# Carrying the last Gram products of a fused attention kernel into the pass over v

## The chip, the cores and the metric

The kernel runs on one core of a Trainium2 chip. Its metric is the device time of one execution in microseconds (us); the time before is 2299.94 us, the median of three runs (2297.13 to 2300.26). The engines are named as the profile names them: PE is TensorE (matmuls, with PEld its weight loads), DVE is VectorE, ACT is ScalarE, POOL is GpSimd, and SP is SyncE, which here only issues transfers. "q" behind a name (SPq, ACTq) is the queue of that engine's sequencer. Each engine works through its own instructions in the order in which they were laid down.

## The reference, cut to what matters

One image `x` of 384 channels and 192 x 192 pixels goes through two residual layers. Only the first is touched by the change:

```python
qkv = einsum('bchw,oc->bohw', groupnorm(x), w_qkv) + b_qkv   # 384 -> 1152 channels
qkv = qkv.reshape(..., 96, 2, 96, 2).max(axis=(3, 5))        # 2x2 max pooling
qkv = depthwise_conv3x3(qkv) + b_dw
q, k, v = split(qkv, 3)                                      # 8 heads of 48 channels
attn = (q/|q|) @ (k/|k|).T * temperature                     # over channels: 48 x 48 per head
out  = sum_i topk_softmax(attn, k_i) @ v * a_i               # k_i = 24, 32, 36, 38
x    = x + w_proj @ upsample2x(gelu(out)) + b_proj
```

The attention is over channels, so q and k are needed only through the 48 x 48 products q k^T of each head (the Gram matrices) and through the norms of their rows. The second layer is a group norm, a sign, a shift by channel and a product with the signs of a weight matrix.

## The kernel before, in words

The image is cut into 24 units of 8 rows (`NU`, 1536 pixels each); a unit of x is a tile of 128 partitions x 3 channel groups x 1536 pixels (2304 KB), held in the pool `big` of 8 buffers. There are four stages.

1. **Statistics** (0 to 160 us): all units are read for the group norm; the last six read stay in SBUF (`kept`).
2. **The q,k pass** (160 to about 1345 us): for each unit u and each of six groups of 128 output channels (m = 0 to 5), `qkv_unit` makes three blocks of 128 x 512 on TensorE (L321; three matmuls a block, each of which shows as two records), VectorE pools each block out of PSUM into a padded tile (L328), ScalarE adds the bias (L335) and makes the first tap of the depthwise convolution (L342), and VectorE makes the other eight taps (L344). Then `transposed` (L381, L384) writes 32 x 32 transposes into the tile `blocks`, and `moved` sends these through 32 transfers on SyncE's queue (L394 for q, L399 for k, sixteen each) into the tile `room`, where they form whole transposed operands. `products(u)` (L410) multiplies them into three PSUM tiles `gram` that accumulate over all units. It is called one unit late, behind m = 2 of the unit after, so that the moves have a good part of a unit to land. Only the last unit has no unit after it: its products are called directly behind its moves, and then L438 copies the Gram tiles to SBUF (`gsb`).
3. **The v pass** (about 1337 to 1990 us): the same for the three groups of v, without transposes; the result goes to `chunk`. From unit 1 on, `softmaxes` (a generator that makes one step after each m) turns the Gram matrices into the attention matrix, and `attention` applies it once it is there. At the start of this stage `w_projG` and `weightT` are loaded into one buffer `wl` one after the other (L574, L580, on ScalarE's queue), VectorE reduces the first (L575), and ScalarE takes the sign of the second (L581).
4. **Projection and second layer** (1990 us to the end).

Pools set much of what may overlap. SBUF pools of the side "right" are a stack: what is opened later takes the memory of what was closed. `p2w` holds the six padded tiles of q and k and `blocks`; when it closes, `p4w` (v's padded tiles and `wl`) and `p3` (the softmax's scratch) take its place, and their first writers wait for the last user of the memory that they take. In PSUM the q,k pass has five buffers for products of x (`p2qkv`) and three for the Gram tiles (`p2g`); the v pass has three (`p4qkv`), four for `attention` (`p4o`) and one for small things (`p3ps`).

Outside the parts written under a manual schedule, a scheduler lays down the order of each engine's instructions from the program's order, its priorities and its own estimate of when an instruction could run; the order in the source is therefore not always the order on the engine.

Of the kernel before, what the change touches and what calls it, by code (L numbers as in the profile page):

```python
# [10 lines left out]
F32 = mybir.dt.float32  # L11
# [7 lines left out]
PSUM = bass.MemoryType.PSUM  # L19

P = 128
C = 384
CT = C // P
# [5 lines left out]
GRP = 12  # L29
NG = C // GRP  # L30
NM = 3 * C // P
UR = 8
NU = H // UR
# [28 lines left out]
KEEP = 6  # L62
# [15 lines left out]
NP = C // PAIR  # L78
# [69 lines left out]
def conv_preact_kernel(ctx: ExitStack, tc: tile.TileContext, a: dict, out: bass.AP):  # L148
    nc = tc.nc
# [27 lines left out]
    def unit(u, pool=big, parts=1):  # L177
        xt = pool.tile([P, CT, UPX], F32, name="xt", tag="big")
        n = CT // parts
        for t in range(0, CT, n):  # L180
            nc.sync.dma_start(xt[:, t : t + n], xv[u][:, t : t + n])
        return xt
# [12 lines left out]
    def group_sums(ps, s):  # L195

        for t in range(CT):
            nc.tensor.matmul(ps, ind[:, t, :], s[:, t], start=(t == 0), stop=(t == CT - 1))  # L198
# [8 lines left out]
    def right(name, bufs=1, stack=att):  # L207
        return stack.enter_context(tc.tile_pool(name=name, bufs=bufs, side="right"))
# [87 lines left out]
    def padded(pool, n):  # L296


        ts = []
        for m in range(n):  # L300
            t = pool.tile([P, PR + 3, WP + 2], F32, name=f"pooled{m}")
            nc.gpsimd.memset(t[:, 0:2, :], 0.0)  # L302
            nc.gpsimd.memset(t[:, 2 : PR + 2, 0:1], 0.0)
            nc.gpsimd.memset(t[:, 2 : PR + 2, WP + 1 :], 0.0)
            nc.gpsimd.memset(t[:, PR + 2 :, :], 0.0)
            ts.append(t)
        return ts
# [38 lines left out]
            nc.scalar.copy(pl[:, 0:2, :], pl[:, PR : PR + 2, :])  # L346


    with tc.tile_pool(name="p2w", bufs=1, side="right") as wp, tc.tile_pool(
        name="p2t", bufs=2, side="right"  # L350
    ) as tp, tc.tile_pool(name="p2qkv", bufs=5, space=PSUM) as pqkv, tc.tile_pool(
        name="p2g", bufs=1, space=PSUM
    ) as pg:
        pool = padded(wp, 2 * CT)
        gram = [pg.tile([P, 512], F32, name=f"gram{t}") for t in range(CT)]


        size = -(-(PR + 1) * WP // P) * C
        blocks = wp.tile([P, 2, size], F32, name="blocks")
        nc.gpsimd.memset(blocks, 0.0)  # L360
        room = big.tile([P, CT, UPX], F32, name="room", tag="big").rearrange("p t n -> p (t n)")
        qkT = room[:, : 2 * size].rearrange("p (s n) -> p s n", s=2)

        def of_unit(u):

            lo, hi = rows(u)
            n = hi - lo + 1
            nk = -(-n * WP // P)
            q, k = qkT[:, 0, : nk * C], qkT[:, 1, : nk * C]
            return (  # L370
                n,
                nk,
                q.rearrange("p (t k c) -> p t k c", t=CT, k=nk),
                k.rearrange("p (b k c) -> p b k c", k=nk, c=B),
            )

        def transposed(u, s, t, acc):
            n, nk, *_ = of_unit(u)
            to = blocks[:, s, : nk * C].rearrange("p (j t k c) -> p t k j c", j=NBP, t=CT, c=B)[:, t]
            full, more = divmod(n * WP // B, NBP)  # L380
            nc.vector.transpose(to[:, :full], acc[:, : full * P].rearrange("p (k j c) -> p k j c", j=NBP, c=B))  # L381
            if more:
                src = acc[:, full * P : n * WP].rearrange("p (j c) -> p j c", c=B)
                nc.vector.transpose(to[:, full, :more], src)  # L384

        def moved(u, s):

            n, nk, q, k = of_unit(u)
            for j in range(NBP):
                src = blocks[:, s, j * nk * CT * B : (j + 1) * nk * CT * B]  # L390
                for i in range(NBP):
                    at, to = slice(i * B, (i + 1) * B), slice(j * B, (j + 1) * B)
                    if s == 0:
                        nc.sync.dma_start(  # L394
                            q[to].rearrange("p t k (i c) -> p i (t k) c", i=NBP)[:, i],
                            src[at].rearrange("p (m c) -> p m c", c=B),
                        )
                    else:
                        nc.sync.dma_start(  # L399
                            k[to].rearrange("p (t i) k c -> p i t (k c)", i=NBP)[:, i],  # L400
                            src[at].rearrange("p (t m) -> p t m", t=CT),
                        )

        def products(u):

            n, nk, q, k = of_unit(u)
            for i in range(nk):
                L = min(P, n * WP - i * P)
                for t in range(CT):
                    nc.tensor.matmul(  # L410
                        gram[t][:, : BN[t] * B],
                        q[:L, t, i],
                        k[:L, B0[t] : B0[t] + BN[t], i],
                        start=u == 0 and i == 0,
                        stop=u == NU - 1 and i == nk - 1,
                    )

        for u in range(NU):
            for v in range(u, min(u + KEEP + 1, NU)):
                if v not in kept:  # L420
                    kept[v] = unit(v)
            xt = kept.pop(u)
            lo, hi = rows(u)
            n = hi - lo + 1
            for m in range(2 * CT):
                acc = tp.tile([P, (PR + 1) * WP], F32, name="dw")[:, : n * WP]
                qkv_unit(pqkv, xt, u, m, pool[m], [(acc, 0, n)])
                transposed(u, *divmod(m, CT), acc)
                sq = tp.tile([P, (PR + 1) * WP], BF16, name="sq", bufs=1)
                nc.scalar.activation(sq[:, : n * WP], acc, AF.Square, accum_out=ssq[:, m, u : u + 1])  # L430
                if u and m == CT - 1:
                    products(u - 1)
                if m % CT == CT - 1:
                    moved(u, m // CT)
        products(NU - 1)
        for t in range(CT):
            at = D0[t] - B0[t] * B
            nc.vector.tensor_copy(gsb[:, t, : DN[t]], gram[t][:, at : at + DN[t]])  # L438

    wpr = ctx.enter_context(tc.tile_pool(name="wpr", bufs=1)).tile([P, CT, C], F32, name="wpr")  # L440
    nc.scalar.dma_start(wpr, a["w_projT"].rearrange("(t p) o -> p t o", p=P))
# [120 lines left out]

    chunk = []
    with ExitStack() as vs:
        wp = right("p4w", stack=vs)
        scratch = vs.enter_context(ExitStack())
        p3 = right("p3", stack=scratch)
        pqkv = vs.enter_context(tc.tile_pool(name="p4qkv", bufs=3, space=PSUM))
        po = vs.enter_context(tc.tile_pool(name="p4o", bufs=NP, space=PSUM))
        psp = vs.enter_context(tc.tile_pool(name="p3ps", bufs=1, space=PSUM))  # L570
        pool = padded(wp, CT)

        wl = wp.tile([P, CT, C], F32, name="wl")
        nc.scalar.dma_start(wl, a["w_projG"].rearrange("(t p) o -> p t o", p=P))  # L574
        nc.vector.tensor_reduce(wg1, wl.rearrange("p t (g c) -> p t g c", c=GRP), AX.X, ALU.add)  # L575
        bg = psp.tile([P, P], F32, name="p3ps")[:NG, :1]
        group_sums(bg, bpr.unsqueeze(2))
        nc.vector.tensor_scalar_mul(bg1, bg, -1.0 / GRP)
        wl = wp.tile([P, CT, C], F32, name="wl")
        nc.scalar.dma_start(wl, a["weightT"].rearrange("(t p) o -> p t o", p=P))  # L580
        nc.scalar.activation(wb, wl, AF.Sign, saturate=False)  # L581
# [20 lines left out]
                    nc.scalar.activation(chunk[c][to, t, cols], ps[src], AF.Gelu, accum_out=osum[to, t, g : g + 1])  # L602

        for u in range(NU):
            xt = unit(u)
            if u == NU - 1:
                kept[u] = xt
                for i, f in enumerate(FIRST):
                    kept[f] = unit(f, big if i else early)
            if u % UC == 0:  # L610
                chunk.append(big.tile([P, CT, CPX], F32, name="chunk", tag="big"))
            lo, hi = rows(u)
            first = PR * u - 2 + lo
            last = first + hi - lo
            for m in range(CT):
                parts = []
                for c in range(first // CR, last // CR + 1):
                    r0, r1 = max(first, c * CR), min(last, c * CR + CR - 1)
                    parts.append(
                        (chunk[c][:, m, (r0 - c * CR) * WP : (r1 + 1 - c * CR) * WP], r0 - first, r1 + 1 - r0)  # L620
                    )
                qkv_unit(pqkv, xt, u, 2 * CT + m, pool[m], parts)
                if u >= TOPK and steps is None:
                    steps = softmaxes(p3, psp)
                if steps:
                    if next(steps, 1):
                        steps = ()
                        scratch.close()
                        early = opened("p5x0", 1)
                elif steps == () and done < NAB - HOLD and (done + 1) * ABLK <= first * WP:  # L630
                    attention(done)
                    done += 1
# [216 lines left out]
```

## Time and profile before

| what | value |
| --- | --- |
| time, median of 3 runs | 2299.94 us |
| span of the profiled execution | 2297.4 us |
| TensorE busy | 2104.5 us, 92% |
| VectorE busy | 1903.4 us, 83% |
| ScalarE busy | 819.2 us, 36% |
| GpSimd busy | 211.2 us, 9% |
| products of x (L321), 3888 records | 1682.8 us |
| depthwise taps (L344) of q, k and of v | 709.1 and 370.7 us |
| pooling (L328), 648 instructions | 443.0 us |
| block moves to `room` | 768 transfers, 2.0 us to landing |

The page's row of slices cuts the span into 40 parts of 57.4 us and gives the busy share of each in tenths. The groups give for each line and operation the busy time, the mean duration of one instruction in ns, and the idle time of the engine just before them with what ended most of it. A timeline lists instructions in order of time, with equal ones that follow each other merged; its bracket has the idle time before and the releaser.

### The profile page before, as it was taken

How to read it: one execution, taken by the hardware profiler on the slowest of the kernel's cores; microseconds unless marked ns; L12 is line 12 of the kernel's file. 1: busy time of each engine (PE TensorE's matmuls, PEld its weight loads, DVE VectorE, ACT ScalarE, POOL GpSimd, SP SyncE). 2: the span in 40 equal slices, each digit the busy share in tenths (PEclk: the TensorE clock that was granted, in tenths of full speed). 3: DMA queues.
4: the chain of work that ended last, by engine and by line, in shares of the span. 5: the costliest groups of instructions: out<-in, count | busy, mean ns of one | idle time of the engine just before them, and what ended most of it. 6: DMA issues, size and time to landing. Idle time of an engine off the chain costs nothing.

```text
span 2297.4 us, 19469 instructions
## 1 busy us (share of the span) xinstructions
PE 2104.5 (92%) x6135; PEld 995.6 (43%) x6135; DVE 1903.4 (83%) x3269; ACT 819.2 (36%) x1418; POOL 211.2 (9%) x338
## 2 busy tenths in 40 slices
PE   1029999999999999999999969999999999989998
PEld 0014444444444444444444434443444444455554
DVE  4658888888888888888888958986787887889998
ACT  5532222222222222222222212225333233487775
POOL 0000000000000000000000000000000000286674
PEclk7559999999999999999999989999999999999999
DMA  9962222222222322222111154104221212289996
GB/s 398 418 256 62 63 65 69 87 80 70 63 67 67 101 69 68 62 69 65 21 27 25 21 175 161 42 2 204 83 82 56 110 42 83 83 330 398 423 414 247
DMA packets 208727, 300.30 MB, mean 131 GB/s; under 512 B 162000, under 2 KB 164848, under 8 KB 208624
## 3 DMA queue, kind: packets, MB, share of 16 engines
q1 hardware_dynamic: 197936, 243.46, 30.4%
q10 hardware_dynamic: 10688, 55.61, 5.9%
q8 instruction: 48, 0.79, 0.1%
q14 instruction: 55, 0.45, 0.1%
HBM read 213.68 MB, written 56.62 MB: 118 GB/s over the span
## 4 chain that ended last, share of the span: by engine, by line
PE 75%; DVE 11%; DMA 9%; ACT 2%; issue 1%; SPq 1%; ACTq 0%; POOLq 0%; POOL 0%; DVEq 0%
PE qkv L321 63%; DMA xt<-in_x_dram 6%; PE l1ps L734 4%; DVE chunk L344 4%; PE yps L552 3%; PE gram L410 3%; DVE pooled L328 2%; PE ops L592 2%; DVE xt L561 2%; DVE dw L344 1%; DMA out_dram<-xt 1%; ACT signs L714 1%; DVE stats L248 1%; DMA wl<-in_weightT_dram 1%; DMA wl<-in_w_projG_dram 1%
## 5 line engine op out<-in xcount | busy, mean ns | idle before, releaser
L321 PE MATMUL qkv<-xt,wq 128*128 128x512 f32 x3888 | 1682.8, 594 | 1.9 <-DVE pooled L328 1.6
L321 PEld LDWEIGHTS qkv<-xt,wq 128*128 128x128 f32 x3888 | 736.4, 190 | 922.4 <-issue 824.5
L344 DVE SCALAR_TENSOR_TENSOR dw<-pooled,small,dw 128x384 f32<-128x384 f32 (+2 forms) x1152 | 709.1, 616 | 118.4 <-ACT dw L342 93.7
L328 DVE TENSOR_REDUCE pooled<-qkv 128x128 f32<-128x512 f32 x648 | 443.0, 685 | 83.2 <-PE qkv L321 71.1
L344 DVE SCALAR_TENSOR_TENSOR chunk<-pooled,small,chunk 128x384 f32<-128x384 f32 (+3 forms) x696 | 370.7, 547 | 77.9 <-ACT chunk L342 60.3
L346 ACT COPY pooled<-pooled 128x196 f32<-128x196 f32 x207 | 73.6, 356 | 773.6 <-DVE dw L344 542.9
L335 ACT ACTIVATE pooled<-pooled,small 128x384 f32<-128x384 f32 x216 | 133.0, 616 | 408.2 <-DVE pooled L328 408.1
L714 ACT ACTIVATE signs<-xt,nmean 64x1536 fp8e4<-64x1536 f32 x144 | 226.5, 1573 | 62.5 <-PE yps L552 51.3
L734 PE MATMUL l1ps<-signs,wb 128*128 128x384 fp8e4 x864 | 151.5, 330 | 6.5 <-POOL signs L706 4.6
L561 DVE SCALAR_TENSOR_TENSOR xt<-yps,small,xt 128x768 f32<-128x768 f32 x132 | 127.9, 1013 | 23.8 <-PE yps L552 20.1
L742 DVE SCALAR_TENSOR_TENSOR xt<-l1ps,small,xt 128x768 f32<-128x768 f32 x144 | 135.7, 1009 | 7.1 <-ACT signs L714 4.0
L552 PE MATMUL yps<-chunk,wpr 128*128 128x384 f32 x396 | 136.5, 490 | 5.3 <-DVE xt L561 5.3
L248 DVE BATCH_NORM_STATS2 stats<-xt 128x6 f32<-128x512 f32 x144 | 87.2, 677 | 60.4 <-DMA xt<-in_x_dram 60.4
L302 POOL MEMSET pooled<- 128x196 f32 x9 | 2.4, 264 | 1351.5 <-DMA room<-blocks 1192.0
L198 PE MATMUL gsps<-sums,small 128*32 128x2 f32 x6 | 0.5, 196 | 128.2 <-DVE sums L269 128.2
L430 ACT ACTIVATE sq<-dw 128x384 bf16<-128x384 f32 (+2 forms) x144 | 75.3, 523 | 116.9 <-DVE dw L344 116.9
L734 PEld LDWEIGHTS <-wb 128*128 128x128 fp8e4 x864 | 84.4, 98 | 74.8 <-issue 17.3
L342 ACT ACTIVATE dw<-pooled,small 128x384 f32<-128x384 f32 (+2 forms) x144 | 100.5, 698 | 2.3
L552 PEld LDWEIGHTS yps<-chunk,wpr 128*128 128x128 f32 x396 | 72.6, 190 | 60.8 <-PE yps L552 16.4
L239 ACT ACTIVATE junk<-xt 128x1536 bf16<-128x1536 f32 x48 | 71.1, 1482 | 52.0 <-DMA xt<-in_x_dram 50.8
L381 DVE STREAM_TRANSPOSE blocks<-dw 128x384 f32<-128x384 f32 (+1 forms) x144 | 82.0, 569 | 3.5
L410 PE MATMUL gram<-room 128*128 128x160 f32 (+3 forms) x438 | 69.9, 315 | 12.4 <-DMA room<-blocks 12.4
(117 smaller groups left out, 642.1 us busy)
## 6 DMA issues: line engine op xcount, KB each, us to landing
xt<-in_x_dram SPq DMA_DIRECT2D x83, 2304.0 KB, 14.9
out_dram<-xt ACTq DMA_DIRECT2D x19, 2304.0 KB, 14.5
room<-blocks SPq DMA_DIRECT2D x736, 36.0 KB, 2.0
xt<-in_x_dram SPq DMA_DIRECT2D x18, 768.0 KB, 8.3
out_dram<-xt ACTq DMA_DIRECT2D x9, 768.0 KB, 8.0
out_dram<-xt SPq DMA_DIRECT2D x6, 768.0 KB, 6.6
wq<-in_w_qkvT_dram ACTq DMA_DIRECT2D x1, 1728.0 KB, 14.9
room<-blocks SPq DMA_DIRECT2D x32, 48.0 KB, 2.0
```

The costliest lines, as they stand in the source:

```text
L248: nc.vector.bn_stats(stats[b][:, t, at : at + 6], xt[:, t, j * 512 : (j + 1) * 512])
L321: nc.tensor.matmul(ps, wq[:, t, m * P : (m + 1) * P], x4[:, t, r0 : r0 + nr, c0 : c0 + ncol], start=(t == 0), stop=(t == CT - 1),)
L328: nc.vector.tensor_reduce(pl[:, 2 + r0 // 2 : 2 + (r0 + nr) // 2, 1 + c0 // 2 : 1 + (c0 + ncol) // 2], ps.rearrange("p (i a j b) -> p i j ...
L335: nc.scalar.activation(new, new, AF.Identity, bias=bq[:, m : m + 1])
L342: nc.scalar.activation(acc2, src, AF.Identity, bias=bdw[:, m : m + 1], scale=wdw[:, m, 0:1])
L344: nc.vector.scalar_tensor_tensor(acc2, src, wdw[:, m, k : k + 1], acc2, ALU.mult, ALU.add)
L410: nc.tensor.matmul(gram[t][:, : BN[t] * B], q[:L, t, i], k[:L, B0[t] : B0[t] + BN[t], i], start=u == 0 and i == 0, stop=u == NU - 1 and i ...
L552: nc.tensor.matmul(ps, wpr[:, t, m * P : (m + 1) * P], o[:, t, :], start=(t == 0), stop=(t == CT - 1),)
L561: nc.vector.scalar_tensor_tensor(x5[:, m, r], yb, bpr[:, m : m + 1], x5[:, m, r], ALU.add, ALU.add)
L714: nc.scalar.activation(rows_of(sg, p, SAT[t] - HSHIFT[t][h]), xt[p, t, :].rearrange("p (r w) -> p r w", w=W), AF.Sign, bias=nmean1[p, t : ...
L734: nc.tensor.matmul(ps[:, j, : 2 * W], wb[:, t, m * P : (m + 1) * P], rows_of(sg, slice(0, P), SAT[t])[:, r0 + 2 * j : r0 + 2 * j + 2], sta ...
L742: nc.vector.scalar_tensor_tensor(blk, ps[:, :, : 2 * W], bl1[:, m : m + 1], blk, ALU.add, ALU.add)
```

## The change

The edit has three parts that belong together.

- **The last unit's products move.** `products(NU - 1)` and the copies of the Gram tiles leave the end of the q,k pass and become a function `gathered`, called in the v pass behind m = 1 of its first unit, so that there is work for TensorE while the last moves are under way. The buffers of the Gram tiles therefore stay open into the v pass, and the pools `p4o` and `p3ps`, with the three small bias sums (`group_sums`), open only behind `gathered`.
- **One PSUM pool for products of x.** A pool `qkv` of three buffers serves both passes in place of `p2qkv` (five) and `p4qkv` (three).
- **v's first tiles and units are freed of the moves.** In `p2w`, `blocks` is laid down ahead of the padded tiles, so that what `p4w` overlaps is padded tiles and not `blocks`; `p4w` gets `reuse_waits="tile"`, by which a new tile waits for the users of the tiles whose memory it takes, not for the whole pool. The loop over x units in the q,k pass reads ahead past its end: the v pass's units 0 to 5 are loaded by its last six rounds and kept under the keys 24 to 29.

```diff
-    with tc.tile_pool(name="p2w", bufs=1, side="right") as wp, tc.tile_pool(
-        name="p2t", bufs=2, side="right"
-    ) as tp, tc.tile_pool(name="p2qkv", bufs=5, space=PSUM) as pqkv, tc.tile_pool(
-        name="p2g", bufs=1, space=PSUM
-    ) as pg:
-        pool = padded(wp, 2 * CT)
+    products_of_x = ctx.enter_context(ExitStack())
+    pqkv = products_of_x.enter_context(tc.tile_pool(name="qkv", bufs=3, space=PSUM))
+    last_products = products_of_x.enter_context(ExitStack())
+    pg = last_products.enter_context(tc.tile_pool(name="p2g", bufs=1, space=PSUM))
...
         blocks = wp.tile([P, 2, size], F32, name="blocks")
         nc.gpsimd.memset(blocks, 0.0)
+        pool = padded(wp, 2 * CT)
...
-            for v in range(u, min(u + KEEP + 1, NU)):
+            for v in range(u, u + KEEP + 1):
                 if v not in kept:
-                    kept[v] = unit(v)
+                    kept[v] = unit(v % NU)
...
+    def gathered():
         products(NU - 1)
         for t in range(CT):
             at = D0[t] - B0[t] * B
             nc.vector.tensor_copy(gsb[:, t, : DN[t]], gram[t][:, at : at + DN[t]])
+        last_products.close()
...
-        wp = right("p4w", stack=vs)
+        wp = vs.enter_context(tc.tile_pool(name="p4w", bufs=1, side="right", reuse_waits="tile"))
...
-        pqkv = vs.enter_context(tc.tile_pool(name="p4qkv", bufs=3, space=PSUM))
-        po = vs.enter_context(tc.tile_pool(name="p4o", bufs=NP, space=PSUM))
-        psp = vs.enter_context(tc.tile_pool(name="p3ps", bufs=1, space=PSUM))
+        vs.enter_context(products_of_x)
...
         for u in range(NU):
-            xt = unit(u)
+            xt = kept.pop(NU + u) if NU + u in kept else unit(u)
...
                 qkv_unit(pqkv, xt, u, 2 * CT + m, pool[m], parts)
+                if u == 0 and m == 1:
+                    gathered()
+                    po = vs.enter_context(tc.tile_pool(name="p4o", bufs=NP, space=PSUM))
+                    psp = vs.enter_context(tc.tile_pool(name="p3ps", bufs=1, space=PSUM))
+                    bg = psp.tile([P, P], F32, name="p3ps")[:NG, :1]
+                    group_sums(bg, bpr.unsqueeze(2))
+                    nc.vector.tensor_scalar_mul(bg1, bg, -1.0 / GRP)
```

More of the change, by code (lines that the diff above doesn't have):

```diff
@@ L346, in qkv_unit @@
             nc.scalar.copy(pl[:, 0:2, :], pl[:, PR : PR + 2, :])
+    products_of_x = ctx.enter_context(ExitStack())
+    pqkv = products_of_x.enter_context(tc.tile_pool(name="qkv", bufs=3, space=PSUM))
+    last_products = products_of_x.enter_context(ExitStack())
+    pg = last_products.enter_context(tc.tile_pool(name="p2g", bufs=1, space=PSUM))
     with tc.tile_pool(name="p2w", bufs=1, side="right") as wp, tc.tile_pool(
         name="p2t", bufs=2, side="right"
-    ) as tp, tc.tile_pool(name="p2qkv", bufs=5, space=PSUM) as pqkv, tc.tile_pool(
-        name="p2g", bufs=1, space=PSUM
-    ) as pg:
-        pool = padded(wp, 2 * CT)
+    ) as tp:
         gram = [pg.tile([P, 512], F32, name=f"gram{t}") for t in range(CT)]
@@ L575, in conv_preact_kernel @@
         nc.vector.tensor_reduce(wg1, wl.rearrange("p t (g c) -> p t g c", c=GRP), AX.X, ALU.add)
-        bg = psp.tile([P, P], F32, name="p3ps")[:NG, :1]
-        group_sums(bg, bpr.unsqueeze(2))
-        nc.vector.tensor_scalar_mul(bg1, bg, -1.0 / GRP)
         wl = wp.tile([P, CT, C], F32, name="wl")
```

## The prediction

> **What bounds the kernel now.** I read the page first: the slices of the span, then the groups.
>
> ```profile
> PE   1029999999999999999999969999999999989998
> L321 PE MATMUL qkv<-xt,wq 128*128 128x512 f32 x3888 | 1682.8, 594 | 1.9 <-DVE pooled L328 1.6
> ```
>
> TensorE is at 9 tenths in nearly every slice from the fourth on; the products of x (L321) are most of it and hardly wait. One hole stands in mid-span, at the 24th slice (57.4 us each). Splitting the span around it gives this table (length, then busy time of TensorE, its weight loads, VectorE, ScalarE, GpSimd; clock, DMA share, GB/s):
>
> ```profile
> 200.00:1340.00 1140.00, 1138.40 (x2927) 537.08 (x2926) 994.47 (x1684) 301.52 (x694) 0.00 (x0) 1.00 0.23 62
> 1340.00:1403.00 63.00, 41.16 (x110) 21.05 (x109) 30.71 (x67) 7.95 (x15) 2.37 (x14) 0.84 0.67 256
> 1403.00:1990.00 587.00, 585.27 (x1683) 252.00 (x1683) 487.73 (x1002) 193.27 (x438) 3.67 (x5) 1.00 0.21 79
> ```
>
> In the q,k pass TensorE is idle 1.6 of 1140 us, in the v pass 1.7 of 587. So TensorE sets the pace of both, VectorE (87% and 83%) rides along, and the only time to win or lose between them is the 21.8 us of idleness from 1340 to 1403, plus whatever slow restarts cost. The timeline of TensorE in that stretch (start, length, instructions, idle time before and its releaser):
>
> ```profile
> 1314.69 20.76 PE L321 MATMUL qkv<-xt,wq 128*128 128x512 f32 x48
> 1337.05 7.99 PE L321 MATMUL qkv<-xt,wq 128*128 128x512 f32 x18 [1.60 <-DVE pooled L328]
> 1357.49 6.04 PE L410 MATMUL gram<-room 128*128 128x160 f32 x24 [12.45 <-DMA room<-blocks]
> 1363.36 1.02 PE L321 MATMUL qkv<-xt,wq 128*128 128x512 f32 x2
> 1371.80 0.48 PE L198 MATMUL p3ps<-small 128*32 128x1 f32 x6 [7.41 <-DVE gsb L438]
> 1372.20 24.39 PE L321 MATMUL qkv<-xt,wq 128*128 128x512 f32 x52
> ...
> 1396.43 0.38 PE L460 MATMUL p3ps<-dg,ones 128*128 128x128 f32 x2
> 1396.65 1.88 PE L321 MATMUL qkv<-xt,wq 128*128 128x512 f32 x4
> 1400.15 0.49 PE L460 MATMUL p3ps<-dg,ones 128*128 128x128 f32 x2 [1.61 <-DVE dg L458]
> ```
>
> Four waits: 1.60 for a PSUM buffer, 12.45 for the last unit's block moves, 7.41 behind the copies of the Gram tiles, and 1.61 (then 0.36 at 1402.72) for VectorE's diagonal tiles. After 1403.05, 226 records follow without a gap. VectorE and the SyncE queue say why the first two long ones last:
>
> ```profile
> 1345.66 10.25 SPq L399 DMA_DIRECT2D room<-blocks  x16
> 1357.66 1.89 DVE L328 TENSOR_REDUCE pooled<-qkv 128x128 f32<-128x512 f32 x3 [11.87 <-DMA room<-blocks]
> 1369.69 1.35 DVE L575 TENSOR_REDUCE wg<-wl 128x96 f32<-128x1152 f32 x1 [8.24 <-DMA wl<-in_w_projG_dram]
> ```
>
> Sixteen moves leave one per 0.64 us and each lands some 2 us later: 1345.66 + 10.25 + 1.4 = 1357.3. VectorE stands 11.87 us because v's pooled tiles reuse the memory of `blocks`, and 8.24 us at the reduction of w_projG, whose load took 12.1 us among six x loads. The Gram copies (L438) stand behind that reduction in VectorE's order, and TensorE's 7.41 us hangs on them.
>
> [...]after the 7.41 us gap, passes start 0.85 us apart instead of 0.43 for about 4 us; after the 12.45 us one, Gram passes start 0.27 to 0.32 apart for 4.8 us, then about 0.15. [...]The trace: 48 KB moves 1.9 to 2.0 us, lone 2304 KB loads 8.0 to 8.7 (median 8.2).[...]
>
> **The change, part by part.** The built order of the changed kernel is the order of before on every engine except around this transition (and the moved x loads). Decisive is TensorE's order there: last unit's q,k blocks, three blocks of v's m=0, the three bias sums (L198), the *first* Gram matmul of the last unit, only then v's m=1, then the other eleven Gram matmuls. So the scheduler leaves the wait for the moves ahead of the v work meant to cover it.
>
> 1. *q,k pass with 3 PSUM buffers instead of 5: 0 us.* A block is 6 passes x 0.43 = 2.57 us. Comparing in the timeline each block's start with the end of the pooling reduction three blocks earlier, over the whole pass, the smallest margin is 2.5 us. VectorE's order in the pass is unchanged, so no wait appears. `blocks` is cleared before the pooled borders instead of after: 2.66 us later for these, from 163.4; their first reader runs at 172.0.
> 2. *Five x loads moved into the last q,k units: 0 us.* They repeat what the pass did up to 1042 us: one lone 8.2 us load per 49 us unit, moves then landing within 2.9 us, and no Gram wait.
> 3. *The 1.60 us PSUM wait: gone, worth 0 us.* With one pool, v's first block follows at 1335.3, and TensorE reaches the Gram matmul at 1335.3 + 7.75 + 0.5 = 1343.5 instead of 1345.0, to wait there longer.
> 4. *The 12.45 us wait: stays, 14 us long.* Its end is set by VectorE's last transpose. Ahead of that VectorE now has the bias scaling (0.14 us), which waits for the sums, done at 1343.6, before VectorE gets to it at 1344.4. The load of w_projG is now released by the first of the last eight moves (about 1353.5) and shares the engines with the last ones: by the 2.9 us worst landing of a move, 0 to 1 us. I take 0.3 in all: release at 1357.8.
> 5. *From release to the first L460.* Before: 1396.43 - 1357.49 = 38.94 us. The work is 24 Gram passes (18 take 2.61 us when warm, so 3.5) and 54 product passes x 0.43 = 23.2: 26.7 us. One cold start remains: 2.4 us lost after the long gap (5.87 against 3.5), 1.9 after the short one; I take 2.2. So 28.9 us, **10.0 us less**. The 7.41 us must not come back, so walk VectorE: the three m=0 reductions are already done by 1348 (their tiles overlap pooled tiles, not `blocks`); the first softmax step still waits for the moves, since p3's tiles do overlap `blocks`. At release come the small softmax steps (1.5 us) and one v step, so at 1360 it reaches the w_projG reduction. That load, alone in the queues, takes 2.0 + 6.2 x 576/2304 = 3.5 us[...] and is there by 1357.5. The Gram copies come late in m=1, when the Gram matmuls have ended at about 1371.5, and nothing of TensorE's queues behind them: the banks that they free are first used in unit 1. The weightT load (issued about 1361.5, landing by 1365.5) no longer holds ScalarE's v bias, which before stood until 1384.9.
> 6. *The 1.61 + 0.36 us for the diagonal tiles.* They arise because VectorE is 2.4 us behind after its stalls. Walked through with 0.6 per reduction and 0.53 to 0.65 per step, VectorE ends the reduction before them 0.7 us after its matmuls; 0 to 0.3 us remains: **1.7 us less**.
> 7. *Later:* the v pass has no idleness to absorb the shift, and loads of the last stage are released by its matmuls, so all moves earlier together.
>
> Sum: 10.0 + 1.7 - 0.3 = 11.4 us; 2299.94 - 11.4 = **2288.5 us**.
>
> **The rivals.**
> - *Half hidden:* TensorE does v's m=1 ahead of the Gram matmuls, as the edit is meant. It would reach them at 1343.5 + 7.75 = 1351.3 and wait 6.5 us: 7.75 better than the forecast, 2280.8. Against it: the built order, which engines keep. (Even then the wait is not gone.)
> - *The weight loads take the place of the removed wait.* If each took 12.1 us also without x loads beside it, ScalarE's Sign of weightT would end near 1380, v's m=1 steps would start then, and the reduction that unit 1's first block needs would be 8 us late: gain 3.4, 2296.5. Against it: lone loads of four times the size take 8.2 us.
> - *Three buffers bind (slower):* VectorE is 87% busy in the q,k pass; had every unit one wait of 1 us, 24 x 1 - 11.4 gives 2312.5. Against it: the 2.5 us margin and the unchanged order.
>
> **How the numbers follow.** Forecast 0.82, half hidden 0.05, late weight loads 0.08, buffers bind 0.05. The forecast's own spread: 0 to 1 us of move delay, 0.5 for the cold start, 0.3 at the diagonals, and some 1.5 us of the measurement (before: 2297.13 to 2300.26); half the late-loads case lies within 2293. Range 2284.5 to 2293. The bound of 0.2% is 4.6 us, 2295.3: faster is forecast, half hidden and the milder late loads, 0.90; same 0.05; slower 0.05.
>
> **What would show it.** After: one TensorE wait of about 14 us before the first Gram matmul, still put down to the moves; none before L198; no wait on the Gram copies; VectorE standing about 10 us for the moves but not for w_projG; that load landing in under 5 us; about 2 us less to wait at the diagonals; no PSUM waits from 200 to 1335. Wrong if the Gram wait is much shorter, if L321 waits for pooling in the q,k pass, or if ScalarE or VectorE stand on a weight load past 1366.

## The result, and the profile after

The changed kernel takes 2287.92 us (median of four runs, 2287.21 to 2288.68), the kernel before beside it 2300.10 (2297.13 to 2300.76): 12.2 us less, a ratio of 0.995 with a 95% interval of 0.9932 to 0.9967. On another chip the same two gave 2288.42 and 2299.40. The forecast was 2288.5.

The page first, the slices of TensorE and the group of the products of x (busy us, mean ns, idle time before them):

```profile
PE   1029999999999999999999979999999999999998
L321 PE MATMUL qkv<-xt,wq 128*128 128x512 f32 x3888 | 1684.0, 594 | 0.3 <-DVE small L294 0.3
```

The hole at the 24th slice has become shallower (7 tenths for 6) and is still there; the products of x now wait 0.3 us in all, and none of it for pooling. The same three stretches as in the prediction (length, then busy time of TensorE, its weight loads, VectorE, ScalarE, GpSimd; clock, DMA share, GB/s):

```profile
200.00:1340.00 1140.00, 1140.00 (x2931) 537.97 (x2930) 994.42 (x1684) 301.14 (x693) 1.05 (x9) 1.00 0.26 73
1340.00:1403.00 63.00, 47.55 (x132) 23.18 (x131) 41.82 (x96) 10.19 (x20) 1.51 (x6) 0.86 0.21 69
1403.00:1990.00 587.00, 584.47 (x1694) 252.90 (x1693) 486.17 (x988) 195.81 (x444) 4.07 (x5) 1.00 0.21 81
```

In the middle stretch TensorE is idle 15.45 us instead of 21.8, and the DMA share fell from 0.67 to 0.21: the loads of x that ran there have been made earlier. TensorE's timeline says which waits went:

```profile
1316.02 28.49 PE L321 MATMUL qkv<-xt,wq 128*128 128x512 f32 x66
1344.44 0.35 PE L198 MATMUL p3ps<-small 128*32 128x1 f32 x6
1360.24 0.87 PE L412 MATMUL gram<-room 128*128 128x160 f32 x2 [15.45 <-DMA room<-blocks]
1360.90 9.90 PE L321 MATMUL qkv<-xt,wq 128*128 128x512 f32 x18
1370.64 3.37 PE L412 MATMUL gram<-room 128*128 128x192 f32 x22
1373.84 15.62 PE L321 MATMUL qkv<-xt,wq 128*128 128x512 f32 x36
1389.29 0.38 PE L467 MATMUL p3ps<-dg,ones 128*128 128x128 f32 x2
...
1393.21 0.49 PE L467 MATMUL p3ps<-dg,ones 128*128 128x128 f32 x2
```

Of the waits before (1.60, 12.45, 7.41, 1.61 and 0.36 us) one is left, and it has grown to 15.45. TensorE comes to the first Gram matmul (L412) with three blocks of v behind it and stands there for the last moves; the second wait, behind the load of `w_projG`, and the two at the diagonals (L467, L460 before) are gone. The queues and the other engines in the same stretch:

```profile
1347.06 10.27 SPq L401 DMA_DIRECT2D room<-blocks  x16
1354.29 0.40 ACTq L579 DMA_DIRECT2D wl<-in_w_projG_dram  x1
1360.22 0.30 DVE L455 TENSOR_REDUCE ss<-ssq 128x6 f32<-128x144 f32 x1 [11.26 <-DMA room<-blocks]
1362.70 1.35 DVE L580 TENSOR_REDUCE wg<-wl 128x96 f32<-128x1152 f32 x1
1367.81 1.16 ACT L583 ACTIVATE wb<-wl 128x1152 fp8e4<-128x1152 f32 x1 [2.90 <-DMA wl<-in_weightT_dram]
```

VectorE still stands 11.26 us for the moves, but the reduction of `w_projG` (L580) follows without any wait. One thing is new: `w_projG` is issued at 1354.29, while the sixteen moves are being issued, and the slowest of these moves now takes 5.0 us to land, against 2.0 at most before:

```profile
DMA to landing us min/median/max: 1.9/2.0/5.0
```

**Where the 10.5 us between the two profiled spans (2297.4 and 2286.9) lie:**

| piece of the span | before | after | difference |
| --- | --- | --- | --- |
| to the Gram products of the last unit but one | 1312.08 | 1313.42 | +1.34 |
| from there to the last unit's first Gram matmul | 45.41 | 46.82 | +1.41 |
| from there to the first diagonal | 38.94 | 29.05 | -9.89 |
| from there to 1403.05 and 1393.53, where the diagonals end and only products of x follow for a while | 6.62 | 4.24 | -2.38 |
| to the end | 894.35 | 893.37 | -0.98 |

The first row isn't the change. Both q,k passes begin with a half-clock phase of TensorE, and it lasted longer in this execution. The 8 us from the first product of x, in the kernel before and then in the changed one (busy time and records of TensorE, of its weight loads, of VectorE; clock, DMA share, GB/s):

```profile
160.85:168.85 8.00, 7.98 (x15) 3.61 (x16) 1.39 (x2) 0.79 0.00 0
```

```profile
160.85:168.85 8.00, 8.00 (x12) 3.44 (x13) 0.69 (x1) 0.62 0.00 0
```

Fifteen records against twelve: three passes of 0.43 us, 1.3 us in all. The full clock came 3.3 us behind the first product before and 6.0 after. The difference comes and goes without the edit: weights_behind, spare_two_queues and two_queues, kernels of the experiments below that begin the pass just as the changed one does, reach the Gram products of the last unit but one at 1312.18, 1312.44 and 1312.97 us, and a second profile of the changed kernel reaches them at 1313.07. Without this difference the traces differ by 11.8 us.

Nor is the last row the change. Up to the first product of the second layer (`l1ps`) the two traces go alike: 606.2 us from the third diagonal in both. Soon after, TensorE waits 3.5 us in both, and the same 34 records behind that wait take 8.31 us before and 7.40 after, with the clock at half for 6.8 and for 3.4 us:

```profile
2019.11 8.31 PE L734 MATMUL l1ps<-signs,wb 128*128 128x384 fp8e4 x34 [3.47 <-POOL signs L706]
```

```profile
2009.56 7.40 PE L743 MATMUL l1ps<-signs,wb 128*128 128x384 fp8e4 x34 [3.46 <-POOL signs L715]
```

That is 0.91 of the 0.98 us. Both rows are slow phases of unlike length (the last section has more on them), and only the three rows between them belong to the transition.

### The profile page after: what moved, and what is told of

Its sections match the earlier page's. It is cut to its first block, busy times and chain, and to the rows that moved or that the text cites. A ratio compares the mean times of both kernels' runs of the same rounds, so it can differ in the third digit from the quotient of the medians.

```text
span 2286.9 us, 19474 instructions
## 1 busy us (share of the span) xinstructions
PE 2101.7 (92%) x6135; PEld 993.8 (43%) x6135; DVE 1903.2 (83%) x3269; ACT 819.4 (36%) x1418; POOL 211.4 (9%) x338
## 4 chain that ended last, share of the span: by engine, by line
PE 78%; DVE 11%; DMA 7%; ACT 2%; issue 1%; SPq 1%; ACTq 0%; POOL 0%; POOLq 0%; DVEq 0%
PE qkv L321 65%; DMA xt<-in_x_dram 7%; PE l1ps L743 5%; DVE chunk L344 4%; PE yps L559 3%; PE gram L412 3%; DVE pooled L328 2%; PE ops L594 2%; DVE xt L568 2%; DVE dw L344 1%; DVE stats L248 1%; DMA out_dram<-xt 1%; ACT signs L723 1%; SPq L401 0%; DVE xt L751 0%
## 5 line engine op out<-in xcount | busy, mean ns | idle before, releaser
L198 PE MATMUL gsps<-sums,small 128*32 128x2 f32 x6 | 0.5, 196 | 128.5 <-DVE sums L269 128.5
L412 PE MATMUL gram<-room 128*128 128x160 f32 (+3 forms) x438 | 68.1, 309 | 15.4 <-DMA room<-blocks 15.4
```

What stands on the lines that cost most here:

```text
L412: nc.tensor.matmul(gram[t][:, : BN[t] * B], q[:L, t, i], k[:L, B0[t] : B0[t] + BN[t], i], start=u == 0 and i == 0, stop=u == NU - 1 and i ...
```

## The experiments

Two theories stood at first. **A**: the gain is the end of TensorE's second wait, behind the load of `w_projG`; the moved products are worth nothing. **B**: it comes from v's work beside the last moves and the last products, as the edit intends. Later runs ask what sets the end of the wait that remains. Kernels of one group ran on one chip, with the kernel before beside them; "less" is against that.

| kernel | time, us | less, us | ratio to before, 95% | wait for the moves, us | from its end to the first diagonal, us |
| --- | --- | --- | --- | --- | --- |
| before (first group) | 2300.14 | | | 12.45 | 38.94 |
| prefetch_only | 2288.30 | 11.8 | 0.9934 to 0.9959 | 12.34 | 29.87 |
| free_only | 2291.51 | 8.6 | 0.9952 to 0.9977 | 13.79 | 29.04 |
| no_prefetch | 2294.23 | 5.9 | 0.9961 to 0.9984 | 15.42 | 33.43 |
| spare_banks | 2283.37 | 16.8 | 0.9915 to 0.9942 | 10.54 | 23.83 |
| before (second group) | 2299.40 | | | | |
| changed_again | 2288.42 | 11.0 | 0.9941 to 0.9966 | 15.37 | 28.94 |
| weights_early | 2289.80 | 9.6 | 0.9943 to 0.9970 | 13.96 | 29.72 |
| two_queues | 2281.69 | 17.7 | 0.9910 to 0.9935 | 9.36 | 28.38 |
| spare_two_queues_early | 2279.01 | 20.4 | 0.9900 to 0.9927 | 4.43 | 23.74 |
| before (third group) | 2300.31 | | | | |
| weights_behind | 2287.76 | 12.6 | 0.9934 to 0.9959 | 14.04 | 29.17 |
| spare_two_queues | 2276.70 | 23.6 | 0.9892 to 0.9922 | 4.53 | 23.46 |
| prefetch_two_queues | 2282.74 | 17.6 | 0.9919 to 0.9944 | 7.80 | 28.71 |

(The 12.45 and 38.94 are from the profile of before; changed_again is the changed kernel, in a second profile of its own.)

### Which part of the change carries the gain

**prefetch_only**: the kernel before, with the read-ahead of x and nothing else.

```diff
-            for v in range(u, min(u + KEEP + 1, NU)):
+            for v in range(u, u + KEEP + 1):
                 if v not in kept:
-                    kept[v] = unit(v)
+                    kept[v] = unit(v % NU)
...
-            xt = unit(u)
+            xt = kept.pop(NU + u) if NU + u in kept else unit(u)
```

> The kernel before, with only its last six rounds of the q,k pass reading ahead, so that the v pass's first x units are in SBUF before the transition. Theory A (the gain is the end of TensorE's second wait, behind the w_projG load; where the products stand is worth nothing): w_projG lands 3.7 us after 1357.6 instead of 12.1, the 7.41 us wait falls to at most 0.5, its cold start (1.9) and the waits for the diagonal tiles (2.0) go too, and the block moves no longer share with that load: 11 us less than before, about 2289. Theory B (the gain comes from v work standing beside the last unit's moves and products): little, 0 to 2 us less than before, about 2299.

The read-ahead alone gave 11.8 us, as much as the whole change. TensorE's timeline of this kernel, in which the last products stand where they stood before:

```profile
1357.86 6.39 PE L410 MATMUL gram<-room 128*128 128x160 f32 x24 [12.34 <-DMA room<-blocks]
...
1365.03 0.35 PE L198 MATMUL p3ps<-small 128*32 128x1 f32 x6
...
1387.73 0.38 PE L460 MATMUL p3ps<-dg,ones 128*128 128x128 f32 x2
```

The Gram matmuls wait as before, and L198, which stood 7.41 us in the kernel before, doesn't wait at all. With no x loads beside it `w_projG` landed in 3.8 us instead of 12.1. VectorE still stood 11.57 us for the moves and TensorE still 1.60 for a PSUM buffer, and neither shows in the time. This is theory A. The times resolve some 3 us; the traces say it more finely. From the Gram products of the last unit but one to the third diagonal it is 90.64 us before, 79.79 in the changed kernel and 79.09 here, so the rest of the change adds 0.7 us.

**free_only**: the kernel before, with `blocks` laid down ahead of the padded tiles and with waits by tile, and nothing else.

```diff
-        pool = padded(wp, 2 * CT)
...
         nc.gpsimd.memset(blocks, 0.0)
+        pool = padded(wp, 2 * CT)
...
-        wp = right("p4w", stack=vs)
+        wp = vs.enter_context(tc.tile_pool(name="p4w", bufs=1, side="right", reuse_waits="tile"))
```

> The kernel before, with only blocks laid ahead of the padded tiles and the tile-wise waits of p4w. Theory A: w_projG's load starts at about 1353.5 and is there in time, so the 7.41 us wait goes (with its cold start 9.3), but the moves land 1.4 us later beside it, and weightT's load runs among five x loads (12.7 us), so ScalarE is held to about 1377 and VectorE's lag leaves some of the diagonal waits: 6 to 8 us less than before, about 2293. Theory B: 0 to 2 us less, about 2299.

It gave 8.6 us, where 6 to 8 were expected. `w_projG` could now be issued at 1353.17 instead of 1357.6, ahead of the x loads, and was there after 4.6 us; so this edit removes the same 7.41 us wait by another way. What it leaves is `weightT`, which still ran among the x loads (12.7 us). ScalarE's timeline:

```profile
1375.91 1.16 ACT L581 ACTIVATE wb<-wl 128x1152 fp8e4<-128x1152 f32 x1 [10.04 <-DMA wl<-in_weightT_dram]
```

Behind that sign stand v's first taps, VectorE gets late, and TensorE waits 1.96 us at a diagonal. The 11.8 and 8.6 don't add up to 20: both pay for one wait.

**no_prefetch**: the changed kernel without the read-ahead; the moved products, the one pool and the freed tiles stay.

```diff
-            for v in range(u, u + KEEP + 1):
+            for v in range(u, min(u + KEEP + 1, NU)):
...
-            xt = kept.pop(NU + u) if NU + u in kept else unit(u)
+            xt = unit(u)
```

> The changed kernel without the reading ahead: x units of v are loaded behind the moves as before. Theory A: w_projG is still in time, but weightT (issued about 1364 among x loads) lands near 1377; ScalarE's bias of v's m=1 waits for its Sign, VectorE's m=1 steps start near 1380 and unit 1's first block waits about 4 us, the diagonals 2 us again: 4 to 6 us slower than the changed kernel, about 2293. Theory B: the products are still moved, so at most 2 us are lost, 2288 to 2290.

5.9 us are left; the kernel is 6.3 us slower than the changed kernel, where 4 to 6 were expected. The sign of `weightT` waits 11.89 us, and the late taps behind it reach TensorE as a wait for pooling at unit 1's first block, with a slow restart behind it:

```profile
1382.91 9.48 PE L321 MATMUL qkv<-xt,wq 128*128 128x512 f32 x18 [3.35 <-DVE pooled L328]
```

The wait is at the place that the expectation named (3.35 for about 4 us); the 2 us at the diagonals did not come. The moved products do not stand in for the read-ahead. Beside free_only, which lacks them and the one PSUM pool, this kernel gains 2.7 us less, though single runs of the two overlap. This is also the prediction's second rival at work, at 2294.2 where that rival said 2296.5; but the loads of `weightT` are slow here because x loads run beside them (12.7 us), and not, as the rival had it, without them (3.7 in the changed kernel).

**spare_banks**: the changed kernel, with two PSUM buffers that are idle at that time given to the first two blocks of v's m = 1, so that TensorE does these ahead of the Gram matmuls, as the edit meant.

```diff
-            ps = pqkv.tile([P, 512], F32, name="qkv")
+            ps = (pmore if pmore and c0 == 0 else pqkv).tile([P, 512], F32, name="qkv")
...
-                qkv_unit(pqkv, xt, u, 2 * CT + m, pool[m], parts)
+                spare = u == 0 and m == 1
+                if spare:
+                    more_products = last_products.enter_context(ExitStack())
+                    pmore = more_products.enter_context(tc.tile_pool(name="qkvx", bufs=2, space=PSUM))
+                qkv_unit(pqkv, xt, u, 2 * CT + m, pool[m], parts, pmore if spare else None)
+                if spare:
+                    more_products.close()
```

> The changed kernel with the two PSUM banks that lie idle at the transition given to the first two blocks of v's m=1, so that TensorE's order has five v blocks ahead of the first Gram matmul instead of three. Theory A (the Gram wait ends when the last move lands, whatever TensorE does before): TensorE comes to the Gram matmul 5.15 us later and finds the same end, so the wait falls from about 15 to 10 us and the time by 5 us, to about 2283. Rival: VectorE, which stands for the moves too (its first softmax step), sets the restart instead, and unit 1 waits for its poolings: the same time as the changed kernel, 2288.

```profile
1359.13 0.87 PE L412 MATMUL gram<-room 128*128 128x160 f32 x2 [10.54 <-DMA room<-blocks]
...
1382.96 0.38 PE L467 MATMUL p3ps<-dg,ones 128*128 128x128 f32 x2
```

The wait is 4.9 us shorter than 15.45 and the time 4.6 us less than the 2287.92: twelve records of 0.43 us, 5.15 us, were done inside the wait. So moved work is worth about its length here once it stands ahead of the waiting instruction. In the changed kernel it stands behind it: with three buffers, v's m = 1 could not begin before VectorE had pooled m = 0, and the first Gram matmul was laid down in between.

### Why the remaining wait ended 1.4 us later

**weights_early**: the changed kernel with both weight loads put into the q,k pass, into columns of `room` that nothing else uses.

```diff
+        wl = room[:, 2 * size : 2 * size + CT * C].rearrange("p (t o) -> p t o", t=CT)
...
+                if u in (1, 2) and m == 0:
+                    nc.scalar.dma_start(wl, a["w_projG" if u == 1 else "weightT"].rearrange("(t p) o -> p t o", p=P))
```

> The changed kernel, with w_projG and weightT loaded and reduced in the q,k pass (units 1 and 2, into columns of room that nothing else uses) instead of at the start of the v pass, so that no other load shares the DMA engines with the last block moves. Theory C (the last moves land 1.4 us late because the w_projG load is released by the first of them and shares the engines): every one of the last moves lands in 1.9 to 2.0 us, TensorE's wait for them ends 1.0 to 1.5 us earlier against the end of the q,k pass, and the time is 0.8 to 1.5 us below the changed kernel's of the same chip, about 2286.7. Rival (the lateness belongs to the moves or to VectorE's order): landings of 3 to 5 us remain and the time is the changed kernel's within 0.5 us.

Half a miss. The last moves all landed in 1.9 to 2.0 us and the wait fell by 1.41 us, from 15.37 to 13.96. But the time was no better than changed_again's, because nothing held the loads back to units 1 and 2. ScalarE's queue:

```profile
142.76 0.38 ACTq L438 DMA_DIRECT2D room<-in_w_projG_dram  x1
154.41 0.37 ACTq L438 DMA_DIRECT2D room<-in_weightT_dram  x1
```

At 142.76 us the statistics stage is still reading x, at a DMA share of 0.96 over its 160 us, and the first product of x came at 163.10 instead of 160.80 us: 2.3 us given away. In the eleven profiles without these early loads it came between 160.74 and 161.00. The order in the source was an order of programming, not of time.

**weights_behind**: the changed kernel with one word altered.

```diff
-        nc.scalar.dma_start(wl, a["w_projG"].rearrange("(t p) o -> p t o", p=P))
+        nc.sync.dma_start(wl, a["w_projG"].rearrange("(t p) o -> p t o", p=P))
```

> The changed kernel with one word altered: w_projG is loaded on SyncE's queue, where it stands behind the last sixteen moves, instead of on ScalarE's queue, where it starts beside them. Each engine's order is otherwise the changed kernel's. Theory C (the w_projG load beside the last moves delays them by 1.4 us): all sixteen land in 1.9 to 2.1 us, TensorE's wait for them is 13.9 to 14.1 us instead of 15.4, VectorE still doesn't wait for w_projG, and the time is 1 to 1.5 us below 2288. Rival: the wait stays above 15 us and the time is 2288 within the measurement.

TensorE's timeline and the landings of the last moves:

```profile
1357.59 0.87 PE L412 MATMUL gram<-room 128*128 128x160 f32 x2 [14.04 <-DMA room<-blocks]
```

```profile
DMA to landing us min/median/max: 1.9/2.0/2.0
```

The wait is 14.04 us, all moves land in 2.0, and VectorE still doesn't wait for `w_projG`, now issued at 1356.2. So the load beside the moves is what delayed them: beside a 576 KB load on the other queue the last 48 KB moves took up to 5.0 us, with the load behind them on their own queue 2.0. How the two queues shared the engines was not shown. From the Gram products of the unit before to the first of the last unit it is now 45.41 us, just as in the kernel before, so the load explains the whole 1.41 us. The kernel takes 12.6 us less than before, the changed one 11.0 and 12.2 in its two measurements; 1.4 us is too little for these intervals, and 2287.76 us is not the 1 to 1.5 below 2288 that was expected: what is shown is the wait, not the time. In the traces the stretch from the Gram products of the last unit but one to the third diagonal is 78.50 us, against 79.79 and 79.60 in the changed kernel's two profiles.

### What sets the end of the wait

**two_queues**: the changed kernel, with every second of the last sixteen moves issued on ScalarE's queue.

```diff
+                    queue = nc.scalar if s and u == NU - 1 and i % 2 else nc.sync
...
-                        nc.sync.dma_start(
+                        queue.dma_start(
                             k[to].rearrange("p (t i) k c -> p i t (k c)", i=NBP)[:, i],
```

> The changed kernel, with every second of the last unit's sixteen moves of k issued on ScalarE's queue, so that eight leave on each queue. Theory D (TensorE's wait for the last moves is set by issuing them one by one, 0.64 us each on one queue): the issue takes about 5.1 us instead of 10.25, the wait ends 4 to 5 us earlier, and the time is about 2283. Rival (the end is set by landing, by the w_projG load beside the moves or by VectorE's transposes): the wait ends at most 2 us earlier and the time is 2286 to 2288.

SyncE's and ScalarE's queues, then TensorE:

```profile
1346.60 5.17 SPq L402 DMA_DIRECT2D room<-blocks  x8
1346.65 5.56 ACTq L402 DMA_DIRECT2D room<-blocks  x8
1352.31 0.55 ACTq L580 DMA_DIRECT2D wl<-in_w_projG_dram  x1
```

```profile
1353.71 0.87 PE L413 MATMUL gram<-room 128*128 128x160 f32 x2 [9.36 <-DMA room<-blocks]
```

6.7 us less than changed_again on the same chip, where the shorter wait was to give 4 to 5. From the first issue to the Gram matmul it is 7.1 us instead of 13.2: 4.7 us of issue time, and 1.4, as in weights_behind, because `w_projG` now stands behind eight moves on its own queue and no longer runs beside them (the sixteen moves land in 1.9 to 2.1 us). The expectation had left out the second. So 4.7 of the 6.1 us are issue time, and there was much of it to save: issuing is 10.3 of the 11.8 us from first issue to release in the kernel before, since sixteen small moves leave one per 0.64 us.

**prefetch_two_queues**: the two edits of prefetch_only and two_queues on the kernel before.

> The kernel before with the x read-ahead and the last moves on two queues, and nothing else: the last products stay in the q,k pass, the PSUM pools and the padded tiles are those of before. Theory A (the read-ahead carries the gain and the moved products are worth nothing, also with a shorter wait): the wait falls by 4.5 to 5 us as it did in the changed kernel, and the time is 2282 to 2284. Rival (the moved products and the freed tiles begin to count once the wait is under 10 us): 2285 or more, with a new wait of VectorE or TensorE behind the Gram matmuls.

It gave 17.6 us, as much as two_queues (17.7). The wait is 7.80 us, and nothing waits behind the Gram matmuls. So the moved products are worth nothing here either, as far as these runs resolve it (73.38 us from the Gram products of the last unit but one to the third diagonal, 73.03 in two_queues): in both kernels TensorE does v's three blocks of m = 0 ahead of the wait, and no more.

**spare_two_queues_early** joins spare_banks, two_queues and weights_early; **spare_two_queues** joins the first two alone.

> All three together on the changed kernel: two idle PSUM banks for the first blocks of v's m = 1 (TensorE works 5 us more ahead of the wait), the last moves on two queues, and the two weight loads in the q,k pass. If the three terms are separate pieces of one wait they add: 4.5 + 4.5 + 1.3 us, about 2277.5, with a wait of 4 to 6 us left. Rival (the shorter wait uncovers another, VectorE's work behind the moves or the diagonal tiles): 2280 or more, and a wait for VectorE shows between the Gram matmuls and the diagonals.

> The changed kernel with the two idle PSUM banks for v's m = 1 and the last moves on two queues, the weight loads left where they are in the changed kernel (behind the moves on ScalarE's queue, so not beside them). In the run with all three edits the q,k pass began 2.2 us later, because the weight loads had come into the statistics stage. Without them: 2279.0 - 2.2 = 2276.8. Rival (the loads at the start of the v pass cost something once the wait is short): 2279 or more, and VectorE or ScalarE waits for a weight load.

The first came to 2279.0 for the expected 2277.5, with the wait at 4.43 us as expected, but the q,k pass began 2.1 us late (162.93), as in weights_early. Without the early loads it is 2276.7, as expected. TensorE of spare_two_queues:

```profile
1353.21 2.05 PE L413 MATMUL gram<-room 128*128 128x160 f32 x6 [4.53 <-DMA room<-blocks]
...
1376.67 0.38 PE L468 MATMUL p3ps<-dg,ones 128*128 128x128 f32 x2
```

VectorE waits 2.3 us for `w_projG` in this kernel, which costs TensorE nothing. This is the best version of the study: 23.6 us less than before, about twice what the change gives.

**changed_again** is the changed kernel once more.

> The changed kernel once more, on the chip of the three beside it, so that differences of one or two microseconds can be read from the same chip. Every theory: 2287 to 2289.

## Why the prediction was right, point by point

1. *Three PSUM buffers cost nothing.* Right: TensorE is busy 1140.00 of 1140 us, and no product of x waits for pooling in the pass.
2. *Five more x loads in the last units cost nothing.* Right, by prefetch_only: no Gram wait in the pass (the sixth x load of the read-ahead waits for a buffer and comes only at 1381.76 us). But the step priced the loads only where they went. Their leaving the v pass was put to work inside step 5, as "alone in the queues", and that alone gives the whole gain. The sum doesn't tell which part of the edit earns its 10.0 us; only the runs do.
3. *The 1.60 us wait is worth nothing.* Right: it still stands in prefetch_only, which is as fast.
4. *The Gram wait stays; the moves end 0.3 us later, at most 1.* The wait was right, 15.45 us for "about 14". **The delay was the mis-sized term: 1.4 us, beyond its bound.** That bound came from the worst landing of a 36 KB move beside a load of x, 2.9 us; a 48 KB move beside `w_projG` took 5.0. The cause, the load beside the moves, was the right one: with the load behind them, in weights_behind, all land in 2.0.
5. *From release to the first diagonal 28.9 us, 10.0 less.* Measured 29.05, 9.9 less. `w_projG` took 5.2 us beside the moves rather than the 3.5 estimated from 2.0 for a small move and 8.2 for a lone load of x (3.8 in prefetch_only, with neither moves nor loads of x beside it); that misses the "under 5" among the signs, but it was still ahead of VectorE.
6. *The diagonals, 1.7 us.* Measured 2.4. The two waits had been taken as the idle times that the profile shows, 1.61 and 0.36 us; by the starts of the records, 2.21 and 0.95 us apart where 0.43 is usual, they cost 2.3. And the 0.3 kept back for a remaining wait did not come.
7. *Nothing later.* 1.0 us less was found behind 1393.53. By the traces it is the shorter slow phase at the start of the second layer, 0.91 us, and so nothing that the change does; no run isolates it.

Steps 4 to 6 come to 10.9 us in the traces for the forecast 11.4: 1.1 us of loss was missed in step 4 and 0.7 us of gain in step 6, which largely cancel. The 1.0 us of step 7 and the 1.3 us of the slower start come on top with opposite signs. So the mechanism was right and the size of its main term too, but that the total came within 0.6 us of the forecast is in part luck.

The rivals: *half hidden* didn't happen in the changed kernel, since TensorE kept to the order laid down: the products of v's m = 1 start at 1360.90, behind the first Gram matmul at 1360.24. spare_banks made two thirds of it happen and got 4.6 of its 7.75 us. *Late weight loads* is what no_prefetch shows. *Buffers bind* never showed.

## What to carry to other kernels

Before moving work to cover a wait, look at where it lands in the engine's own order: work that stands behind the waiting instruction covers nothing (the products of v's m = 1 ran only behind the Gram wait of 15.45 us), and here the part meant as a help, the read-ahead, carried everything. When a wait hangs on many small transfers from one queue, count their issue time and the loads that start beside the last of them; a second queue for half of them, with the big load behind and not beside them, took 6 us from this wait. Loads of two passes met at the transition between them (`w_projG` took 12.1 us among six loads of x and 3.8 without them), so ask of each whether it could be made in a pass whose DMA engines have room (their share in the q,k pass is 0.26 with the loads of x in it), and make sure that something holds it there.

## What the runs showed of the hardware

The half-clock phase after idleness isn't of one length. At the start of the same q,k pass, products of x stayed 0.85 us apart for 3.4 us in the kernel before and for 6.1 in the changed one. Behind the wait for the moves, the same 18 products of x took 9.18 us in no_prefetch, 9.90 in the changed kernel and 10.56 in weights_early, against 7.89 at the full clock (no_prefetch, from 1371.67). So a slow restart cost these products 1.3 to 2.7 us, and two executions can differ by more than 1 us by that alone, as the two q,k passes do.

In free_only such a phase followed a shorter wait. Four products of x took 1.88 us ahead of the wait of 1.96 us at a diagonal, which ended at 1392.20, and 2.59 us behind it. By stretches (length, then TensorE's busy time and records; clock, DMA share, GB/s):

```profile
1385.00:1391.00 6.00, 5.25 (x14) 1.00 1.02 417
1394.00:1397.30 3.30, 3.30 (x7) 0.55 0.04 15
1397.30:1403.00 5.70, 5.70 (x14) 1.00 0.00 0
```

The wait of 1.61 us in the kernel before, which ended at 1400.15, had no slow phase behind it: the clock was 1.00 from 1400.10 to 1410.00. What decides between the two was not shown.
